# Second sorting of tokens by expert: its products made in four parts between slot tiles

## The chip, the cores and the metric

The kernel runs on one NeuronCore of one Trainium2 chip. A core has five engines that work side by side, each through its own instructions in order: TensorE (PE, matrix products into the accumulator memory PSUM), VectorE (DVE), ScalarE (ACT), GpSimd (POOL, which here issues the indirect transfers), and SyncE (SP, which issues other transfers). They wait for each other through semaphores. The metric is the device time of one execution in microseconds; smaller is better.

## The reference

Two transformer layers run over 2 x 2048 tokens of width 512, each an attention against 128 context rows and a feed-forward part. The change concerns the last part alone, a layer in which each token goes through one of eight experts:

```python
def _L1_ffn_ref(x, Wg, bg, We, be):
    B, S, D, E = (4, 2048, 512, 8)
    probs = jax.nn.softmax(x @ Wg + bg, axis=-1)
    idx = jnp.argmax(probs, axis=-1)
    p = jnp.take_along_axis(probs, idx[..., None], axis=-1)[..., 0]
    e_idx = idx % We.shape[0]
    h = jax.nn.relu(jnp.einsum('bsd,edf->besf', x, We) + be[None, :, None, :])
    onehot = jax.nn.one_hot(e_idx, We.shape[0], dtype=x.dtype)
    out = jnp.einsum('besf,bse->bsf', h, onehot) * p[..., None]
    return out
...
x = x + _L1_ffn_ref(_layernorm(x, axis=-1), ...)
```

The expert of a token is the place of its largest logit, modulo 8; only that expert's result is used.

## The kernel before

The 4096 tokens are 32 token tiles of 128. Instead of all experts for all tokens, the kernel sorts the tokens by expert into slot tiles of 128 slots each, so that a slot tile has one expert, and computes one product of 128x512 by 512x512 for each. Some slots stay empty; 39 slot tiles always suffice. The sorting is done twice: the first covers token tiles 0 to 21 and gives slot tiles 0 to 14, while the attention of the last token tiles still runs; the second covers all 32 token tiles and gives slot tiles 15 to 38. It can begin only when the last token's expert is known, so it runs beside the products of slot tiles 5 to 11.

The function `routing` is a generator that stops at each `yield`; what lies between two of these is called a step here. The steps of the second sorting are:

1. on PE, the rank of each token among those of its expert (`prank`) and the counts (`pcnt`); on VectorE their copies (L1061, L1063)
2. first slot of each expert (L1077 to L1081, "base")
3. the expert of each slot tile, `te` (L1085 to L1092)
4. the slot of each token, split into slot tile and place in it (L1096 to L1102)
5. and 6. the column masks `ohj`, half the token tiles at a time (L1111 to L1118)
7. to 10. the place masks `ohs` for 8 token tiles each: one comparison of 128x1024 elements on VectorE (L1124), the "comparison 1" to "comparison 4" of this text
11. on PE, 32 products (L1132), one per token tile, that add up in one PSUM tile `pid` (128x48) the token number of each slot; on VectorE, from it, the rows for the gather and the output (L1134 to L1138)

Step 11 takes a PSUM tile from a pool of four banks that slot tiles use too.

The order is written by hand, as each engine works through its instructions in program order. The loop over slot tiles at L1322 takes some steps of the sorting and then issues one slot tile, `expert(j)`. Which steps come ahead of which slot tile is in a small table there. `expert(j)` issues, in this order:

- on POOL, the gather of the rows of slot tile j+4 from `x_dram` into one of six buffers (L1149). From j=11 on this needs the rows of the second sorting
- the turning of slot tile j+1: for even tiles by PE (`pt`, L116) and a copy on ScalarE (L1175); for odd tiles above 4 by a transposing transfer that SP has issued earlier (L829) and a copy on ScalarE (L832)
- on PE, the product `pz` of slot tile j (L1185, four blocks, eight matmul records)
- on VectorE, the centring of slot tile j+3 (L104); for odd tiles also the planes for the transposing transfer (L1161, L826)
- on ScalarE, the activation (L1188), on VectorE the sum with the input (L1189), on POOL the indirect output (L1190)

So on VectorE the centring of tile j+3 stands ahead of the sum of tile j, and on ScalarE the copy for tile j+1 ahead of the activation of tile j.

Of the kernel before, what the change touches and what calls it, by code (L numbers as in the profile page):

```python
# [11 lines left out]
F32 = mybir.dt.float32  # L12
# [12 lines left out]
P = 128  # L25
B, S, T, D = 2, 2048, 128, 512
ND = D // P
NT = B * S // P
# [35 lines left out]
def two_layers(ctx: ExitStack, tc: tile.TileContext, a, out):  # L64
    nc = tc.nc
# [85 lines left out]
    with ExitStack() as l0:  # L151
        w0 = l0.enter_context(tc.tile_pool(name="w0", bufs=1))
        psm = l0.enter_context(tc.tile_pool(name="psm", bufs=2, space=PSUM))
# [333 lines left out]
        with tc.manual_schedule(engines={E.PE, E.DVE, E.Activation, E.Pool}):  # L487
# [20 lines left out]
            for u in range(nu + 2):  # L508
# [34 lines left out]
                if g in (0, NG - 1) and u > 1:  # L543
                    if makes and not loaded:
                        load_, args, _, _ = makes[0]
                        loaded.append(load_(*args))
                    elif makes:
                        _, _, make, args = makes.pop(0)
                        turns[u + 1] = make(loaded.pop(), *args)
                        if makes:  # L550
                            load_, args, _, _ = makes[0]
# [85 lines left out]
    with ExitStack() as up:  # L637
        psm = up.enter_context(tc.tile_pool(name="psm_ff", bufs=2, space=PSUM))
# [99 lines left out]
        for blk in range(NT // NBF):  # L738
            for i in range(NI):
                pg = psg.tile([P, BF], F32, name="pg")  # L740
                pu = psg.tile([P, BF], F32, name="pu")
                for w, dst in ((wgT, pg), (wuT, pu)):
                    for c in range(ND):
                        nc.tensor.matmul(  # L744
                            dst, w[:, c, i * P : (i + 1) * P], xqTs[blk][:, c, :],
                            start=(c == 0), stop=(c == ND - 1),
# [13 lines left out]
                n = (blk + 1) * NBF + t  # L760
# [3 lines left out]
                if i >= 3 and i % 2 == 1:  # L764
                    n = (blk + 1) * NBF + (i - 3) // 2
# [18 lines left out]
    psm = l1.enter_context(tc.tile_pool(name="psm_l1", bufs=4, space=PSUM))  # L784
# [31 lines left out]
    scs, xTs, qTs, keeps, ss_, sums, pTs_, os_ = {}, {}, {}, {}, {}, {}, {}, {}  # L816
# [200 lines left out]
    def part(n, shape, dtype=F32, at=0):  # L1017

        size = math.prod(shape)
        v = xw[n][:, at : at + (size * mybir.dt.size(dtype) + 3) // 4]  # L1020
        if dtype is not F32:
            v = v.bitcast(dtype)[:, :size]
        if len(shape) == 1:
            return v
        names = "abc"[: len(shape)]
        return v.rearrange(f"p ({' '.join(names)}) -> p {' '.join(names)}", **dict(zip(names, shape)))
# [6 lines left out]
    def along(k):  # L1033

        return part(16, [NE], at=NE * k)
# [14 lines left out]
    def routing(first):  # L1050

        nt, nj = (NTA, NJA) if first else (NT, NJB)
# [12 lines left out]
        if first:  # L1065
# [3 lines left out]
            start = along(6)  # L1069
# [36 lines left out]
        ohjs, h = [], nt // 2  # L1106
        for q in range(2):
            n0 = q * h
# [8 lines left out]
            )  # L1117
            nc.vector.tensor_scalar(ohj[:, :, 1, :], ones_j, iota_p, None, ALU.mult)  # L1118
            yield
        ohss = []  # L1120
        for n0, n in zip(range(0, nt, 8), (15, 17, 20, 23)):
            h = min(8, nt - n0)
            ohs = part(n, [h, P], BF16)
# [3 lines left out]
            )  # L1127
            ohss += [ohs[:, i] for i in range(h)]
            yield
        pi = psm.tile([P, 2, nj], F32, name="pid", tag="m")  # L1130
        for n in range(nt):
            nc.tensor.matmul(pi, ohss[n], ohjs[n], start=(n == 0), stop=(n == nt - 1))  # L1132
        tokf, pif = part(16, [nj], at=320), part(16, [nj], at=352)
        nc.vector.tensor_scalar(pif, pi[:, 1, :], float(NT * P), None, ALU.add)  # L1134
        nc.vector.scalar_tensor_tensor(tokf, pi[:, 0, :], float(P), pif, ALU.mult, ALU.add)
# [41 lines left out]
    def expert(j):  # L1177

        te, tok, _ = tile_of[j]
        gathered(j + 4)  # L1180
        turned_x2(j + 1)
        e = nc.tensor.value_load(te, min_val=0, max_val=NE - 1)
        pz = psm.tile([P, D], F32, name="pz", tag="m")
        for c in range(ND):
            nc.tensor.matmul(pz, ring[j][:, c, :], we[:, bass.ds(e, 1), c, :], start=(c == 0), stop=(c == ND - 1))  # L1185
        centered_x(j + 3)
        x, acc = xw[j % 6], part(12 + j % 3, [D])
        nc.scalar.activation(acc, pz, AF.Relu, scale=x[:, D + 2 : D + 3])  # L1188
        nc.vector.tensor_tensor(acc, acc, x[:, :D], ALU.add)  # L1189
        nc.gpsimd.indirect_dma_start(  # L1190
            out=out_rows, out_offset=bass.IndirectOffsetOnAxis(ap=tok, axis=0),
            in_=acc, in_offset=None, bounds_check=NT * P - 1, oob_is_err=False,
        )
# [32 lines left out]
    for n in range(NT):  # L1226
# [67 lines left out]
        if n == NTA + 2:  # L1294
            route = routing(True)
# [22 lines left out]
    gated(NT - 1)()  # L1318
    expert(4)
    route = routing(False)  # L1320
    for j in range(5, NJ):
        for _ in range({5: 1, 6: 2, 7: 1, 11: 1}.get(j, 2)):  # L1322
            next(route, None)
        expert(j)
    sched.close()
# [40 lines left out]
```

## Time and profile before

| what | us |
|---|---|
| median of 3 runs | 1606.68 (1604.94 to 1608.51) |
| profiled execution, its own time | 1610.21 |
| its span | 1608.5 |
| PE busy | 1549.8 (96%) |
| VectorE busy | 1194.1 (74%) |
| ScalarE busy | 723.5 (45%) |
| GpSimd busy | 594.3 (37%) |
| second sorting, from the ranks' product to the token rows | 1464.6 to 1493.5 |
| slot tiles 5 to 38 on PE | 1465.7 to 1598.5 |

The profile is of one execution. Its span runs from the first to the last instruction; its own time is 1.7 us longer. In a timeline, each line gives the start and the duration in us, the engine, the source line, the operation, the tiles written and read, and how many instructions were put together; the bracket at the end gives the time for which the engine stood idle before it, and what released it. Matmul records overlap, so a group's end is a little later than the next one's start. A wait for several semaphores is put down to the one that came last by the profile, which can be the wrong one.

The stretch round the second sorting on ScalarE, as a first example of such lines:

```profile
1484.01 0.69 ACT L1188 ACTIVATE x<-pz,x 128x512 f32<-128x512 f32 x1 [2.60 <-PE pz L1185]
1487.31 1.34 ACT L832 COPY x<-x 128x1024 uint16<-128x1024 uint16 x1 [2.61 <-DVE x L104]
1488.52 0.67 ACT L1188 ACTIVATE x<-pz,x 128x512 f32<-128x512 f32 x1
```

These are the activation of slot tile 9, the copy for slot tile 11, and the activation of slot tile 10.

### The profile page before, as it was taken

How to read it: one execution, taken by the hardware profiler on the slowest of the kernel's cores; microseconds unless marked ns; L12 is line 12 of the kernel's file. 1: busy time of each engine (PE TensorE's matmuls, PEld its weight loads, DVE VectorE, ACT ScalarE, POOL GpSimd, SP SyncE). 2: the span in 40 equal slices, each digit the busy share in tenths (PEclk: the TensorE clock that was granted, in tenths of full speed). 3: DMA queues.
4: the chain of work that ended last, by engine and by line, in shares of the span. 5: the costliest groups of instructions: out<-in, count | busy, mean ns of one | idle time of the engine just before them, and what ended most of it. 6: DMA issues, size and time to landing. Idle time of an engine off the chain costs nothing. (4 is left out here: it accounts for less than half of the span.)

```text
span 1608.5 us, 26141 instructions
## 1 busy us (share of the span) xinstructions
PE 1549.8 (96%) x9542; PEld 907.2 (56%) x9542; DVE 1194.1 (74%) x2336; ACT 723.5 (45%) x1537; POOL 594.3 (37%) x576
## 2 busy tenths in 40 slices
PE   7999999999999999999999989999999998999997
PEld 5655555555555556544444456666666665654443
DVE  3467777777777885689986587888888889767442
ACT  1222222222222222244336566777777776753343
POOL 2232222222222221110006653566666443544553
PEclk9999999999999999999999999999999999999999
DMA  9511211211111320466768743122111221114563
GB/s 331 174 37 40 47 40 47 43 53 41 47 40 41 74 43 1 150 171 186 184 167 290 252 159 106 34 47 41 47 47 34 41 41 28 40 47 131 158 162 88
DMA packets 180571, 150.90 MB, mean 94 GB/s; under 512 B 97089, under 2 KB 144665, under 8 KB 180444
## 3 DMA queue, kind: packets, MB, share of 16 engines
q1 hardware_dynamic: 170188, 127.25, 28.3%
q0 software_dynamic: 6240, 18.70, 3.9%
q10 hardware_dynamic: 4016, 3.29, 1.0%
q8 instruction: 76, 1.25, 0.3%
q14 instruction: 51, 0.42, 0.1%
HBM read 89.97 MB, written 41.79 MB: 82 GB/s over the span
## 5 line engine op out<-in xcount | busy, mean ns | idle before, releaser
L419 ACT ACTIVATE pr<-sc 128x1024 f32<-128x1024 f32 x64 | 65.6, 1025 | 421.2 <-PE sc L414 421.1
L393 PE MATMUL pq<-xnT,wq 128*128 128x256 f32 x1024 | 254.4, 391 | 0.0
L451 PE MATMUL pw<-wo,att 128*128 128x512 f32 x512 | 230.8, 593 | 0.0
L393 PEld LDWEIGHTS pq<-xnT,wq 128*128 128x128 f32 x1024 | 184.4, 189 | 67.1 <-issue 44.0
L923 POOL TENSOR_TENSOR s<-s,rs 128x1024 f32<-128x1024 f32 x64 | 132.2, 2075 | 165.4 <-DVE rs L922 165.4
L914 ACT ACTIVATE s<-s,mx 128x128 f32<-128x128 f32 x512 | 175.9, 390 | 29.6 <-DVE mx L905 24.8
L403 POOL TENSOR_TENSOR q<-rt,rt 128x256 f32<-128x256 f32 x64 | 46.7, 729 | 339.7 <-DVE rt L402 335.3
L451 PEld LDWEIGHTS pw<-wo,att 128*128 128x128 f32 x512 | 96.9, 190 | 96.4 <-issue 89.9
L441 DVE RECIPROCAL rd<-sc 128x256 f32<-128x256 f32 x64 | 112.4, 1757 | 46.7 <-PE sc L435 46.7
L1185 PE MATMUL pz<-we,x 128*128 x312 | 140.3, 602 | 2.0 <-ACT x L832 1.7
L872 PE MATMUL pq<-xT,wq 128*128 128x256 f32 x512 | 122.6, 382 | 0.0
L955 PE MATMUL pw<-wo,oT 128*128 128x512 f32 x256 | 115.2, 592 | 1.7 <-issue 1.7
L978 PE MATMUL pl<-wgate,xnT 128*128 128x512 f32 x256 | 116.7, 599 | 0.0
L872 PEld LDWEIGHTS pq<-xT,wq 128*128 128x128 f32 x512 | 96.0, 190 | 33.1 <-issue 20.6
L398 DVE TENSOR_TENSOR rt<-pq,rope_cos 128x256 f32<-128x256 f32 x64 | 27.0, 421 | 104.3 <-PE pq L393 104.3
L749 ACT ACTIVATE gate<-pg,gsc 128x512 f32<-128x512 f32 x88 | 60.7, 689 | 93.5 <-PE pg L744 82.8
L900 DVE SCALAR_TENSOR_TENSOR s<-sc,keep 128x1024 f32<-128x1024 f32 x64 | 78.0, 1219 | 26.9 <-PE sc L892 20.6
L1185 PEld LDWEIGHTS pz<-we,x 128*128 128x128 f32 x312 | 58.2, 192 | 69.6 <-issue 65.9
L92 DVE BATCH_NORM_STATS2 st<-x 128x6 f32<-128x512 f32 x130 | 89.3, 687 | 5.6 <-DMA x<-in_ctx 3.4
L744 PE MATMUL pu<-xqT,wuT 128*128 128x512 bf16 x352 | 90.3, 379 | 2.3 <-DVE h L752 2.2
L744 PE MATMUL pg<-xqT,wgT 128*128 128x512 bf16 x352 | 90.3, 379 | 0.0
L810 PE MATMUL py<-wdT,hb 128*128 128x512 bf16 x352 | 78.8, 383 | 2.2 <-DVE hb L804 1.4
(221 smaller groups left out, 2777.5 us busy)
## 6 DMA issues: line engine op xcount, KB each, us to landing
h_dram<-h SPq DMA_DIRECT2D x88, 256.0 KB
hq<-h_dram SPq DMA_DIRECT2D x31, 704.0 KB
x_dram<-x SPq DMA_DIRECT2D x32, 258.0 KB
x<-in_x SPq DMA_DIRECT2D x32, 256.0 KB
we<-in_L_ffn_We SPq DMA_DIRECT2D x8, 1024.0 KB
xnT<-in_x_turned SPq DMA_DIRECT2D x14, 512.0 KB
along<-stat_dram SPq DMA_DIRECT2D x14, 256.0 KB
w_in<-in_L_ffn_w_gate SPq DMA_DIRECT2D x11, 256.0 KB
```

The source lines that it names most:

```text
L92: nc.vector.bn_stats(out=st, in_=x)
L393: nc.tensor.matmul(pq, wqs[c // 2][:, c % 2, par, g * P : (g + 1) * P], xnTs[k][:, c, :], start=(c == 0), stop=(c == ND - 1))
L441: nc.vector.reciprocal(rd, sc[:, 0, B0:])
L451: nc.tensor.matmul(pw, atts[u][:, f, t * P : (t + 1) * P], wo[:, 2 * g + f, :], start=(g == 0 and f == 0), stop=(g == NG - 1 and f == 1),)
L744: nc.tensor.matmul(dst, w[:, c, i * P : (i + 1) * P], xqTs[blk][:, c, :], start=(c == 0), stop=(c == ND - 1),)
L810: nc.tensor.matmul(py, hbs[n][:, i, :], wdT[:, i, :], start=(i == 0), stop=(i == NI - 1))
L872: nc.tensor.matmul(pq, wq1[:, c, f * P : (f + 1) * P], xTs[blk][:, c, :], start=(c == 0), stop=(c == ND - 1))
L914: nc.scalar.activation(s[:, h, :], s[:, h, :], AF.Exp, bias=mx[:, h : h + 1], **accum)
L923: nc.gpsimd.tensor_tensor(s, s, rs.unsqueeze(2).to_broadcast([P, 8, T]), ALU.mult)
L955: nc.tensor.matmul(pw, os_[n][:, c, :], wo1[:, c, :], start=(c == 0), stop=(c == ND - 1))
L978: nc.tensor.matmul(pl, xn2T[n][:, c, :], wgate[:, c, :], start=(c == 0), stop=(c == ND - 1))
L1185: nc.tensor.matmul(pz, ring[j][:, c, :], we[:, bass.ds(e, 1), c, :], start=(c == 0), stop=(c == ND - 1))
```

## The change

Two things change, both for the second sorting alone.

The 32 products are no longer made together in step 11. After each pause that follows a comparison, the products of the comparisons made before that one are issued: comparison 1's eight products come ahead of comparison 3, comparison 2's ahead of comparison 4, and the rest in step 11. They go into a part of the last token tile's scores in PSUM (its second bank), which nothing uses by then, and not into a tile of the pool. The first sorting does as before.

The table of steps changes as well: ahead of slot tiles 5 to 11 came 1, 2, 1, 2, 2, 2 and 1 steps; now it is 2, 2, 2, 1, 1, 1 and 2. Both need eleven steps and end ahead of slot tile 11, whose gather needs the rows.

```diff
-        ohss = []
+
+        ohss, made = [], 0
+        pi = None if first else scs[NT - 1][:, 1, 0, : 2 * nj].rearrange("p (i j) -> p i j", i=2)
         for n0, n in zip(range(0, nt, 8), (15, 17, 20, 23)):
             h = min(8, nt - n0)
             ohs = part(n, [h, P], BF16)
...
             ohss += [ohs[:, i] for i in range(h)]
             yield
-        pi = psm.tile([P, 2, nj], F32, name="pid", tag="m")
-        for n in range(nt):
-            nc.tensor.matmul(pi, ohss[n], ohjs[n], start=(n == 0), stop=(n == nt - 1))
+            for i in range(made, made if first else n0):
+                nc.tensor.matmul(pi, ohss[i], ohjs[i], start=(i == 0), stop=False)
+                made = i + 1
+        if first:
+            pi = psm.tile([P, 2, nj], F32, name="pid", tag="m")
+        for i in range(made, nt):
+            nc.tensor.matmul(pi, ohss[i], ohjs[i], start=(i == 0), stop=(i == nt - 1))
...
     for j in range(5, NJ):
-        for _ in range({5: 1, 6: 2, 7: 1, 11: 1}.get(j, 2)):
+        for _ in range({8: 1, 9: 1, 10: 1}.get(j, 2)):
             next(route, None)
         expert(j)
```

By source order, VectorE gets comparison 1 ahead of slot tile 8, comparison 2 ahead of 9, comparison 3 ahead of 10 and comparison 4 ahead of 11. PE gets eight products ahead of slot tile 10 and 24 ahead of slot tile 11.

## The prediction

> **What bounds the kernel now.** I read the page first, then the engine timelines of the only stretch that the change touches (the second sorting, 1464 to 1494 us), and last the waits after it.
>
> ```profile
> PE 1549.8 (96%) x9542; PEld 907.2 (56%) x9542; DVE 1194.1 (74%) x2336; ACT 723.5 (45%) x1537; POOL 594.3 (37%) x576
> ```
>
> TensorE is busy 96% of the span, so time is lost where PE stands still. The timeline of PE round the second sorting (start, duration, line, tiles, count, and in brackets the idle time and its releaser):
>
> ```profile
> 1480.37 7.03 PE L1185 MATMUL pz<-we,x 128*128 x16
> 1487.24 0.56 PE L1132 MATMUL pid<-x,x 128*128 128x48 bf16 x16
> 1489.09 0.37 PE L1132 MATMUL pid<-x,x 128*128 128x48 bf16 x8 [1.28 <-DVE x L1124]
> 1490.22 0.37 PE L1132 MATMUL pid<-x,x 128*128 128x48 bf16 x8 [0.76 <-DVE x L1124]
> 1490.44 0.63 PE L116 MATMUL pt<-ident,x 128*128 128x128 f32 x4
> 1491.19 8.78 PE L1185 MATMUL pz<-we,x 128*128 x16
> 1499.81 0.60 PE L116 MATMUL pt<-ident,x 128*128 128x128 f32 x4
> 1500.25 7.03 PE L1185 MATMUL pz<-we,x 128*128 x16
> ```
>
> Each run of 16 pz matmuls is two slot tiles, 7.03 us, or 3.43 a tile from start to start. Between tile 10 (ends at 1487.24) and the transposes for tile 12 (1490.44) stand the 32 matmuls of the sorting: 3.20 us, of which 2.04 is waiting for the third and fourth slot comparison (L1124). The 16 pz after it take 8.78 instead of 7.03: 1.75 us more. The table by stretches says why (columns: stretch, length, PE, PEld, DVE, ACT, POOL, granted clock, DMA share, GB/s):
>
> ```profile
> 1492.00:1493.00 1.00, 1.00 (x2) 0.34 (x1) 0.99 (x3) 0.00 (x0) 0.42 (x1) 0.50 0.26 102
> 1495.00:1498.00 3.00, 3.00 (x8) 1.33 (x7) 1.24 (x2) 1.42 (x2) 0.88 (x1) 1.00 0.70 210
> ```
>
> The clock was 0.50 from about 1491 to 1494.5. So the sorting costs PE 2.04 us of waiting, and 1.75 of half clock behind it. Why the comparisons are late is on VectorE:
>
> ```profile
> 1483.88 0.69 DVE L1189 TENSOR_TENSOR x<-x,x 128x512 f32<-128x512 f32 x1
> 1484.48 2.35 DVE L1124 TENSOR_TENSOR x<-t,x 128x1024 bf16<-128x1024 bf16 x2
> 1486.75 0.54 DVE L104 TENSOR_SCALAR x<-x 128x512 f32<-128x512 f32 x1
> 1487.21 0.69 DVE L1189 TENSOR_TENSOR x<-x,x 128x512 f32<-128x512 f32 x1
> 1487.81 2.35 DVE L1124 TENSOR_TENSOR x<-t,x 128x1024 bf16<-128x1024 bf16 x2
> 1490.65 0.67 DVE L104 TENSOR_SCALAR x<-x 128x512 f32<-128x512 f32 x1 [0.48 <-PE pid L1132]
> ```
>
> VectorE works without a gap here. The last two comparisons stand behind tile 9's sum (L1189), not behind tile 10's. The centring of tile 13 (L104, 1490.65) is put down to PE, but it needs tile 13's gathered rows; those were issued here:
>
> ```profile
> 1484.85 1.75 POOL L1190 DMA_INDIRECT out_x<-x,x  x1 [2.33 <-DVE x L1189]
> 1486.90 1.24 POOL L1149 DMA_INDIRECT x<-x_dram,x  x1 [0.30 <-issue]
> 1489.16 1.90 POOL L1190 DMA_INDIRECT out_x<-x,x  x1 [1.02 <-DVE x L1124]
> ```
>
> The gather of tile 13 (1486.90) ends its issue at 1488.14; 1490.65 is 2.5 us later, as for tiles 14 and 15 (1492.42 to 1495.01, 1495.88 to 1498.50). I read the wait as the landing. Last, the waits from 1500 to 1600 us:
>
> ```profile
> DVE x L104 <- DMA x<-x_dram,x: 51.0, 23, 4.0
> POOL out_x L1190 <- DMA out_x<-x,x: 20.1, 11, 2.5
> ```
>
> From about 1505 VectorE waits for nearly every gather, about 2.2 us each, while PE waits 1.8 us in all. The ring sum, output, gather of the tile five on, centring, sum turns in about 7.57 us per two tiles (outputs at 1503.34 and 1529.84, seven tiles on: 3.79 a tile), PE needs 7.3. The tail follows this ring, and the ring was last started by PE: sums 11 and 12 (1497.30, 1500.73) waited for the activations behind pz 11 and pz 12. What delays pz 11 delays the end.
>
> **What the Trainium skill says.** "TensorE: Matmul & The Clock Gate", Part 1: after an idle window of some 3.4 us the clock is halved, and one busy window restores it; the window runs free. The trace agrees: 0.50 for about 3.4 us after a stretch with 2.04 of 3.20 us waited. "SBUF — State Buffer", "SBUF: two separate sides": VectorE in some modes and GpSimd lock a shared port against each other, and descriptors issued from GpSimd suffer. It fits: the outputs during L1124 took 1.75 and 1.90 us against 1.02 elsewhere. "DMA: Bandwidth & Descriptors", "Anatomy of one DMA": some 2.0 us fixed plus bytes over 436 GB/s; for 128x516 floats, 264 KB, an estimate of 2.6 us. The trace's 2.5 us is used.
>
> **The change part by part.** No instruction goes or comes; the 32 products still cost PE about 0.9 us in all. The bank (the second of the last token tile's scores) has been free since VectorE masked those scores, long before, so I charge nothing; at worst one semaphore wait, below 0.1 us. Leaving the pool of four banks out frees one rotation step: PE waits for no bank here, nothing. What counts is the order. Before, VectorE's steps ahead of tiles 5 to 11 are 1, 2, 1, 2, 2, 2, 1; after, 2, 2, 2, 1, 1, 1, 2. So comparisons 1, 2, 3 and 4 come ahead of tiles 8, 9, 10 and 11, and the fourth now stands behind the centring of tile 13 and the sum of tile 10. The last 8 products, ahead of tile 11 on PE, wait for it.
>
> By hand, with start-to-start costs from the timeline: base 1.73 us, tile experts 0.93, positions 3.02, both column masks 2.97, one comparison 1.14, centring 0.45, centring with planes 1.48 (1.37 for tile 11), sum 0.60.
> - Copies of ranks end at 1466.74, base 1468.47, centring 8; sum 5 waits for its activation (1470.12) and ends the step at 1470.73. Experts and positions to 1474.68, centring 9 to 1476.16, sum 6 to 1476.76, masks to 1479.73.
> - Centring 10 ends at 1480.27. PE wanted it at 1479.94: it starts some 0.4 us late. Tile 9's planes leave 1.3 us later than before (1476.3 against 1475.02); with the same 3.27 us to the copy L832, pz 9 starts near 1480.95 instead of 1480.37. This 0.6 us is swallowed by the later stall.
> - Sum 7 to 1480.78, comparison 1 to 1481.92, centring 11 to 1483.29, sum 8 to 1483.89, comparison 2 to 1485.03.
> - GpSimd: output 7 at 1481.15 to 1482.2-1482.9 (1.02 or 1.75 us), gather 12 to 1483.5-1484.4, output 8 to 1485.3-1486.4, gather 13 to 1486.6-1487.7. Landing 2.5 us later: rows 12 at 1486.0-1486.9, rows 13 at 1489.1-1490.2.
> - VectorE: centring 12 and sum 9 to 1487.1-1488.0, comparison 3 to 1488.2-1489.1, then a wait for rows 13; centring 13 with planes to 1490.6-1491.7, sum 10 to 1491.2-1492.3, comparison 4 done (1.22 us) at 1492.4-1493.5.
> - PE: 8 products ahead of tile 10 (0.22 us, no wait), tile 10 to about 1488.1, 16 products to 1488.5, then idle until 1492.5-1493.6. Before, the last 8 started at 1490.22. Later by 2.3 to 3.4 us; I take 3.0, as the outputs do overlap comparisons.
>
> So two waits of 2.04 us together become one of 4 to 5 us. The half clock stays: an idle stretch longer than a window can hardly go unseen. It costs 1.75 again, or up to a second half window (1.7) more; I take 0.7 more. Queued behind the last products on PE are transposes of tile 12 and pz 11; behind comparison 4 on VectorE the token rows (0.6 us), gather 15 and centring 14. Row and gather 15 come at about 1493.9 (before 1494.90), so they are not late. SP's plane transposes move with L826: tile 9 +1.3, tile 11 -0.5, tile 13 -1.5 to -0.4 us; only tile 9's was seen on PE.
>
> The sum: +3.0 +0.7 = +3.7 us on the profiled execution (1610.21 us, span 1608.5), all of it ahead of pz 11 and so carried by the ring to the end. It would make 1613.9 of that one; the same shift on the median of 1606.68 gives 1610.4. The two differ by 3.5 us already, about the spread of the runs (1604.94 to 1608.51), so about 0.2%, 3.2 us, is what counts as a change.
>
> **The rivals.**
> A, the forecast, late fourth comparison: +2.3 to +5.1, 1609.0 to 1611.8. For it: comparison 4's place behind sum 10, which no landing can lift.
> B, rows 13 come early: if they land before comparison 3 ends, only activation 10 holds: pz 10 ends 1488.1, activation to 1488.9, sum 1489.5, comparison 1490.7. PE restarts +0.5, idle 2.2 us in one piece as now in two; if the free window then doesn't see it, the half clock goes: +0.5 -1.75 = -1.2, 1605.5. This is the case not slower; it decides when gather 13 lands before about 1488.4. Against it: output 8 cannot start before 1484.26, and its 1.02, the gather's 1.3 and 2.5 us give 1489.1.
> C, the ring gains what PE loses: output 11 took 5.07 us to release output 12, and rows 16 landed 4.6 us after their issue against 2.5. If outputs 9 and 10, now 1 to 2 us earlier, clear the queue for these, up to 2.1 us of that and PE's 1.8 of later waits come back: +3.7 -3.9 = -0.2, 1606.5; with the half clock gone too, 1604.7 or below. Against it: output 11 itself starts after pz 11.
> That the products are not split at all is excluded by the instruction order.
>
> **How the numbers follow.** A 0.70, B 0.13, C 0.17. Over +3.2 lie three quarters of A, 0.53, and 0.03 of odd delays in the others: slower 0.56. Faster than -3.2 only what B and C reach with the clock gone and an earlier ring: 0.14. The rest, 0.30, is within 0.2%. Eight in ten: 1605.0 to 1613.0, from C's and B's better halves to A with a full second slow window and some spread; A's own range is 1609.0 to 1611.8.
>
> **What would show it.** Right: one PE idle of 3.5 us or more ahead of the last 8 products, released by the comparison; a DVE wait for x_dram ahead of centring 13; clock 0.50 after it; pz 11 near 1493.5 to 1494.5; and no wait at the first 24 products. Wrong: an idle below 2.3 us there, clock 1.00 throughout, or a tail whose sums 13 and on come earlier against pz 11 than now (before, 9.3 us from activation 11 at 1496.58 to sum 13 at 1505.90).

## The result, and the profile after

The changed kernel took 1612.94 us (median of 6 runs, 1610.97 to 1614.74), the kernel before, run again beside it, 1606.21 (1604.94 to 1608.51). The ratio is 1.0043 (95% interval 1.0033 to 1.0053): slower by 6.7 us between the medians, 6.9 by the ratio, where 3.7 had been forecast. The profiled execution took 1612.53 us, its span 1610.8.

The timeline of PE in the changed kernel, round the second sorting (same columns as before):

```profile
1483.20 0.36 PE L1133 MATMUL sc<-x,x 128*128 128x48 bf16 x8
1483.40 3.68 PE L1191 MATMUL pz<-we,x 128*128 x8
1486.92 0.36 PE L1133 MATMUL sc<-x,x 128*128 128x48 bf16 x8
1487.70 0.37 PE L1133 MATMUL sc<-x,x 128*128 128x48 bf16 x8 [0.42 <-DVE x L1126]
1492.62 0.50 PE L1138 MATMUL sc<-x,x 128*128 128x48 bf16 x8 [4.55 <-DVE x L1126]
1492.95 1.09 PE L116 MATMUL pt<-ident,x 128*128 128x128 f32 x4
1493.98 9.00 PE L1191 MATMUL pz<-we,x 128*128 x16
```

The products are in four groups of eight, as the change says: one ahead of slot tile 10, three behind it. The last group waits 4.55 us for comparison 4, where before there were two waits of 1.28 and 0.76. The 16 pz after it take 9.00 us, against 8.78 in the first profile of before and 7.03 at full clock.

The timeline of VectorE in the changed kernel shows why comparison 4 is late:

```profile
1486.42 1.22 DVE L1126 TENSOR_TENSOR x<-t,x 128x1024 bf16<-128x1024 bf16 x1
1489.14 0.55 DVE L104 TENSOR_SCALAR x<-x 128x512 f32<-128x512 f32 x1 [1.50 <-DMA x<-x_dram,x]
1489.72 0.38 DVE L1167 TENSOR_SCALAR x<-x 128x4 f32<-128x4 f32 x1
1490.13 0.69 DVE L826 COPY x<-x 128x1024 uint16<-128x1024 uint16 x1
1490.74 0.68 DVE L1195 TENSOR_TENSOR x<-x,x 128x512 f32<-128x512 f32 x1
1491.35 1.22 DVE L1126 TENSOR_TENSOR x<-t,x 128x1024 bf16<-128x1024 bf16 x1
```

Comparison 3 is done at 1487.64. Then VectorE stands still for 1.50 us until the rows of slot tile 13 land, centres that tile, makes its planes, adds up tile 10, and only then makes comparison 4. Before, VectorE had no gap there and made comparison 4 ahead of all this.

The table by stretches for the changed kernel (stretch, length, PE, PEld, DVE, ACT, POOL, granted clock, DMA share, GB/s):

```profile
1491.00:1492.00 1.00, 0.00 (x0) 0.00 (x0) 1.00 (x2) 0.00 (x0) 0.29 (x1) 0.50 0.67 219
1495.00:1496.00 1.00, 1.00 (x3) 0.48 (x2) 0.00 (x0) 0.00 (x0) 0.57 (x1) 0.50 0.00 0
1498.00:1499.00 1.00, 1.00 (x4) 0.43 (x3) 0.00 (x0) 0.00 (x0) 0.00 (x0) 1.00 0.00 0
```

The number after POOL's is the clock: it is 0.50 already while PE still waits, and is back at 1.00 only near 1497.8. PE worked about 5 us at half speed.

### The profile page after: what moved, and what is told of

It reads as the page before. It is cut to its first block, busy times and chain, and to the rows that moved or that the text cites. A ratio compares the mean times of both kernels' runs of the same rounds, so it can differ in the third digit from the quotient of the medians.

```text
span 1610.8 us, 26141 instructions
## 1 busy us (share of the span) xinstructions
PE 1549.5 (96%) x9542; PEld 906.6 (56%) x9542; DVE 1196.3 (74%) x2336; ACT 721.6 (45%) x1537; POOL 593.3 (37%) x576
## 5 line engine op out<-in xcount | busy, mean ns | idle before, releaser
L914 ACT ACTIVATE s<-s,mx 128x128 f32<-128x128 f32 x512 | 175.2, 388 | 29.2 <-DVE mx L905 24.4
```

The costliest lines, as they stand in the source:

```text
L914: nc.scalar.activation(s[:, h, :], s[:, h, :], AF.Exp, bias=mx[:, h : h + 1], **accum)
```

## How executions are compared here

The second sorting starts with the ranks' product (L1056). Over all profiles it started between 1463.2 and 1468.2 us, although nothing ahead of it differs in any kernel below. That scatter of 5 us has nothing to do with the change, and it is about as large as the effect. So the profiles are compared from this product on: to the transposes for slot tile 12 (PE is past the sorting), to those for tile 14 (past the slow clock), and to the end of the span. All in us, read from the PE timelines and the spans. The last column gives the ratio of the times to those of the kernel before, run on the same chip, with its 95% interval:

| kernel | to tile 12 | to tile 14 | to the end | half clock behind the sorting | timed against before |
|---|---|---|---|---|---|
| before, first profile | 25.8 | 35.2 | 143.9 | yes | |
| before, `x1_before_again` | 25.3 | 33.0 | 141.4 | no | 0.9999 (0.9990 to 1.0009) |
| before, `z1_before_b` | 25.9 | 33.6 | 141.8 | no | |
| before, `z2_before_c` | 25.6 | 33.3 | 144.3 | no | |
| changed | 29.8 | 39.6 | 147.6 | yes | 1.0043 (1.0033 to 1.0053) |
| changed, `y1_after_again` | 29.2 | 39.4 | 148.3 | yes | 1.0035 (1.0023 to 1.0046) |
| `x4_table_only` | 29.2 | 38.8 | 147.7 | yes | 1.0037 (1.0025 to 1.0049) |
| `y2_split_only` | 28.0 | 35.5 | 145.4 | ahead of tile 12 | 1.0011 (1.0004 to 1.0019) |
| `y3_c4_early_split` | 26.4 | 34.2 | 144.6 | no | 1.0001 (0.9993 to 1.0010) |
| `x3_fill_after` | 29.6 | 36.9 | 146.0 | no | 1.0030 (1.0018 to 1.0042) |
| `x2_fill_before` | 25.9 | 33.6 | 143.5 | no | 1.0000 (0.9992 to 1.0007) |
| `y4_all_early` | 24.0 | 31.8 | 142.2 | no | 1.0000 (0.9990 to 1.0011) |
| `z3_deep_gather` | 25.4 | 33.2 | 144.1 | no | 1.0015 (1.0008 to 1.0022) |
| `z4_deep_all_early` | 24.0 | 31.8 | 146.3 | no | 1.0017 (1.0010 to 1.0023) |

## The experiments

### Which part of the change costs it

The theory was the forecast's own: comparison 4 now stands behind the sum of slot tile 10. The rivals were the split products with their bank, and the earlier steps of the sorting. Three kernels part them.

The table alone, on the kernel before:

```diff
-        for _ in range({5: 1, 6: 2, 7: 1, 11: 1}.get(j, 2)):
+        for _ in range({8: 1, 9: 1, 10: 1}.get(j, 2)):
```

> The new table of steps alone: the 32 products together ahead of slot tile 11, in a bank of the pool as before. Theory 'it is comparison 4's place behind the sum of slot tile 10': as slow as the changed kernel, 1612.9 within 1 us, with PE idle about 4.3 us ahead of the last eight products. Rival 'the split products or their bank cost it': near the kernel before, below 1608.

It took 1614.69 us beside 1608.79 for the kernel before on that chip, ratio 1.0037. On its PE timeline the products stand together again, and the wait is there as well, 3.50 us after one of 1.01:

```profile
1491.59 0.56 PE L1132 MATMUL pid<-x,x 128*128 128x48 bf16 x16
1493.17 0.37 PE L1132 MATMUL pid<-x,x 128*128 128x48 bf16 x8 [1.01 <-DVE x L1124]
1497.04 0.50 PE L1132 MATMUL pid<-x,x 128*128 128x48 bf16 x8 [3.50 <-DVE x L1124]
1498.25 8.82 PE L1185 MATMUL pz<-we,x 128*128 x16
```

So the table alone makes the loss, within the intervals all of it; neither the four parts nor the bank are needed for it. The long wait is shorter than the 4.3 us expected, the two together are 4.5. The absolute time was above the 1 us band that was written down, because the kernel before was 2.6 us higher on this chip too; the ratio is what agrees.

The split alone, the changed kernel with the old table (the diff above reversed):

> The products in four parts in the scores' bank, with the old table of steps. Theory 'only the places of the comparisons count': comparison 2 is made late, so PE waits ahead of slot tile 10 (about 2.5 us) and hardly ahead of tile 11; in sum about 0.5 us later than before at tile 11, so within 0.1% of before. Rival 'the split itself costs the 4 to 7 us': as slow as the changed kernel.

Ratio 1.0011 (1.0004 to 1.0019), about 1.8 us slower and at the edge of the 0.1% expected. PE waits at another place:

```profile
1485.11 0.37 PE L1133 MATMUL sc<-x,x 128*128 128x48 bf16 x8 [1.44 <-DVE x L1126]
1486.24 0.50 PE L1133 MATMUL sc<-x,x 128*128 128x48 bf16 x8 [0.76 <-DVE x L1126]
1487.08 4.92 PE L1191 MATMUL pz<-we,x 128*128 x8 [0.34 <-issue]
```

These are the groups of comparisons 1 and 2 ahead of slot tile 10. With the old table those comparisons are not made yet, so PE stands 2.2 us there, and tile 10 runs at half clock in part (4.92 us against 3.6). In exchange the last 16 products wait for nothing. Tile 12 comes 2.3 us later than the mean of before (25.67), not 0.5: the half clock in tile 10, 1.3 us of it, had been left out of the expectation. Splitting the products brings the wait forward; it doesn't shorten it by itself.

The changed kernel with comparison 4 one place earlier:

```diff
-        for _ in range({8: 1, 9: 1, 10: 1}.get(j, 2)):
+        for _ in range({8: 1, 9: 1, 11: 1}.get(j, 2)):
```

> The changed kernel with one edit: comparison 4 is made together with comparison 3 ahead of slot tile 10, so it stands behind the sum of tile 9 and not of tile 10 (table 2, 2, 2, 1, 1, 2, 1). Theory 'comparison 4 behind sum 10 costs it': the idle ahead of tile 11 falls below 1 us, PE waits about 1 us for comparison 2 ahead of tile 10, no half clock: 4 us or more faster than the changed kernel, same as or up to 2 us faster than before. Rival 'the earlier steps (masks ahead of tile 7) delay the tiles': still over 2 us slower than before.

Ratio 1.0001 (0.9993 to 1.0010): the whole loss is gone with one step moved. Its PE timeline:

```profile
1488.44 0.37 PE L1133 MATMUL sc<-x,x 128*128 128x48 bf16 x8 [0.37 <-DVE x L1126]
1489.75 3.70 PE L1191 MATMUL pz<-we,x 128*128 x8 [0.94 <-issue]
1493.28 0.36 PE L1133 MATMUL sc<-x,x 128*128 128x48 bf16 x8
1493.87 0.37 PE L1138 MATMUL sc<-x,x 128*128 128x48 bf16 x8 [0.22 <-DVE x L1126]
```

The last wait is 0.22 us. The masks ahead of tile 7 and the split are still as in the changed kernel, so the rival that these delay the tiles falls as well. It is not faster than before, though: PE now loses 0.37 and 0.94 us ahead of tile 10.

### What the half clock adds

The changed kernel unchanged, on the chip of the runs above:

> The changed kernel, unchanged, on the same chip as the three below. Timed 0.25 to 0.45% slower than before (about 4 to 7 us). The profile again shows one idle of 4 to 5 us ahead of the last eight products and the half clock behind it; from the ranks' product to the transposes for tile 14 about 39.6 us.

Nearly as expected: 1615.78 us beside 1609.88, ratio 1.0035, and half clock behind the wait; the wait is in two pieces, 3.49 us ahead of the last eight products after one of 0.95. From the transposes for tile 12 to those for tile 14 it took 10.15 us, the first profile 9.86; at full clock the same stretch takes 7.69 (`x1_before_again`). Against that, the half clock costs 2.2 to 2.5 us there, and a further 0.1 in the last products and transposes ahead of it.

To take the clock's part away and leave the wait, five 128x512 fp32 products into an unused bank fill it, in the changed kernel:

```diff
+        for _ in range(0 if first else 5):
+            nc.tensor.matmul(scs[NT - 1][:, 2].rearrange("p c k -> p (c k)"), ident, we[:, 0, 0, :], start=True, stop=True)
         for i in range(made, nt):
```

> The changed kernel with five such products (4.3 us) in the 4.55 us in which PE waits for comparison 4. The wait stays; the clock should stay at 1.00. Theory 'one late comparison, and the half clock behind it': 2.4 to 2.7 us faster than the changed kernel, about 1610.4, and still 4 us slower than before. Rival 'the clock is no part of it, the tail takes it up': as the changed kernel, 1612.9.

```profile
1490.16 4.54 PE L1138 MATMUL sc<-we,ident 128*128 128x512 f32 x10
1494.53 0.36 PE L1140 MATMUL sc<-x,x 128*128 128x48 bf16 x8
1494.74 0.64 PE L116 MATMUL pt<-ident,x 128*128 128x128 f32 x4
1495.21 7.03 PE L1193 MATMUL pz<-we,x 128*128 x16
```

The 16 pz take 7.03 us again and the clock is 1.00. The filling ran 0.7 us longer than the wait, which here ended at 1493.8; still tile 14 comes 2.6 us earlier than the mean of the two profiles of the changed kernel (36.9 against 39.5), and the end 1.9 us earlier. The time says less: 1.0030 (1.0018 to 1.0042) against 1.0035 and 1.0043 is 0.8 to 2.1 us faster where 2.4 to 2.7 had been expected, and the intervals overlap. So the clock's part is shown in the profile, and the timed runs neither confirm nor refute its size.

The same in the kernel before, one product ahead of comparison 3's and one ahead of comparison 4's:

```diff
         for n in range(nt):
+            if not first and n in (16, 24):
+                nc.tensor.matmul(scs[NT - 1][:, 2].rearrange("p c k -> p (c k)"), ident, we[:, 0, 0, :], start=True, stop=True)
             nc.tensor.matmul(pi, ohss[n], ohjs[n], start=(n == 0), stop=(n == nt - 1))
```

> The kernel before with one 128x512 fp32 product (0.86 us, into a bank nothing reads) ahead of comparison 3's and one ahead of comparison 4's products, where PE waits 1.28 and 0.76 us. The waits stay, the idle time falls below 0.5 us. If the half clock of 1.75 us is there in the timed executions of the kernel before: 1.3 to 1.75 us faster, about 1604.7, and clock 1.00 behind the sorting. If it is only in the profiled one: same as before within 0.3 us.

Ratio 1.0000 (0.9992 to 1.0007): no gain. That fits a half clock that is mostly absent in the kernel before, which the next runs show directly.

### What the kernel before really does there

> The kernel before, unchanged, for a second profile of it. Timed: ratio 1.000 within 0.1%. Theory 'clock differs between executions' (the half clock behind the second sorting is there in some executions of the kernel before and not in others): this profile may show clock 1.00 from 1491 to 1494.5 and then a profiled time 2 us or so below 1610.21. Rival 'the excess of the first profile lies ahead of the sorting': the stretch from the ranks' product to the transposes for tile 14 again takes about 35.2 us with the half clock in it, and the 3 to 4 us by which the first profile lay above the median are found before 1464 us.

> The kernel before, unchanged, a third profile. So far one of two profiles of it had the half clock behind the products (from the ranks' product to the transposes for tile 14: 35.2 us with it, 33.0 without). If it is chance where the window falls, this one has either; if the first profile was the odd one, 33 us.

> The kernel before, unchanged, a fourth profile, with the same question as the third.

None of the three has the half clock. The third profile (`z1_before_b`) is the telling one, as its waits are as long as those of the first:

```profile
1490.83 0.37 PE L1132 MATMUL pid<-x,x 128*128 128x48 bf16 x8 [1.36 <-DVE x L1124]
1491.96 0.37 PE L1132 MATMUL pid<-x,x 128*128 128x48 bf16 x8 [0.76 <-DVE x L1124]
1492.18 0.64 PE L116 MATMUL pt<-ident,x 128*128 128x128 f32 x4
1492.90 7.13 PE L1185 MATMUL pz<-we,x 128*128 x16
```

2.12 us of waiting, and the 16 pz at full speed; the first profile waited 2.04 us and had 8.78. So with two us of idle time in two pieces the half clock comes in some executions (one of four here) and not in others. With 4.4 to 5.0 us, in two pieces too, it came in each of the three profiles that left the wait unfilled.

What differs is where the waits fall on a time grid. Each trace records when the granted clock changes. Within one trace, any two of these moments are a whole multiple of 3.413 us apart, to within 4 ns; from one execution to the next, this grid lies differently over the work. Cut into windows along the grid (same columns as in the table by stretches above), the first profile of before gives:

```profile
1487.72:1491.13 3.41, 1.31 (x24) 0.88 (x20) 2.93 (x4) 1.47 (x2) 2.32 (x2) 1.00 0.31 90
1491.13:1494.55 3.42, 3.36 (x4) 1.51 (x5) 2.23 (x8) 0.69 (x1) 2.03 (x2) 0.50 0.57 168
```

and `z1_before_b`:

```profile
1487.45:1490.87 3.42, 2.06 (x22) 0.98 (x21) 3.42 (x5) 1.82 (x2) 2.13 (x2) 1.00 0.61 148
1490.87:1494.28 3.41, 2.56 (x23) 1.51 (x24) 2.97 (x5) 0.75 (x2) 2.95 (x2) 1.00 0.35 135
```

In the first, both waits fall into one window, PE is busy for only 1.31 us of it, and the next window has the half clock. In `z1_before_b` a boundary of the grid lies between the two waits; PE is busy for 2.06 and 2.56 us, and the clock stays. The same cut over all 14 profiles, from 30 to 1585 us, finds 43 windows at full clock that have the half clock in the next one. PE was busy for at most 1.77 us in each of them; between 1.52 and 1.77 us the clock dropped in some windows and stayed in others, and every full-clock window with more work was followed by full clock. In the changed kernel the long wait spans a boundary:

```profile
1487.56:1490.97 3.41, 0.37 (x8) 0.27 (x8) 1.84 (x5) 0.78 (x2) 1.99 (x2) 1.00 0.49 156
1490.97:1494.38 3.41, 1.76 (x13) 1.46 (x14) 2.67 (x7) 0.24 (x1) 1.75 (x1) 0.50 0.78 182
```

The second of these windows is itself at half clock, and PE still works for only 1.76 us in it. Another window at half clock follows (in the 14 profiles that happened after half-clock windows with up to 2.65 us of work), so the clock is low for 6.83 us and not for 3.41. The Trainium skill ("TensorE: Matmul & The Clock Gate", Part 1) describes such a free-running window of some 3.4 us, and the traces agree. It names an idle window as what halves the clock; here the clock was halved after windows in which PE worked for up to 1.77 us, and the measurement decides.

### Can another order beat both?

If the wait costs, making the comparisons early enough should pay. With the products together as before, all comparisons two tiles earlier:

```diff
-        for _ in range({5: 1, 6: 2, 7: 1, 11: 1}.get(j, 2)):
+        for _ in range({10: 0, 11: 1}.get(j, 2)):
```

> The products together as before, with all four comparisons two tiles earlier (table 2, 2, 2, 2, 2, 0, 1): comparisons 1 and 2 ahead of tile 8, 3 and 4 ahead of tile 9. Theory: no wait and no half clock at the products, 2 to 3.8 us less than before on PE at tile 11; if the tail keeps that, 0.1 to 0.2% faster than before. Rival 'the tail's ring of gather, centring, sum and output sets the end': the gain at tile 11 is there but gone at the last tile, same as before.

```profile
1490.13 0.97 PE L1132 MATMUL pid<-x,x 128*128 128x48 bf16 x32
1490.94 0.63 PE L116 MATMUL pt<-ident,x 128*128 128x128 f32 x4
1491.73 7.13 PE L1185 MATMUL pz<-we,x 128*128 x16 [0.17 <-ACT x L832]
```

All 32 products run without a wait, in 0.97 us, and tile 12 comes at 24.0 us, 1.7 before the mean of the kernel before. But the ratio is 1.0000 (0.9990 to 1.0011), which leaves room for 1.6 us at most: by the median the gain is lost on the way to the end, as the rival had it.

Two more kernels asked which link of the tail swallows it. From slot tile 15 on, the rows of a tile are gathered six tiles ahead instead of four, into twelve buffers (`xw` 26 to 31 and 0 to 5) instead of six:

```diff
+    def rows(j):
+        return xw[j % 6] if j < NJA else xw[(26 + (j - NJA) % 12) % 32]
...
-        gathered(j + 4)
+        for i in [j + 4] if j < 11 else [2 * j - 7, 2 * j - 6] if j < 13 else [j + 6]:
+            gathered(i)
```

> The kernel before with the gathers six slot tiles ahead instead of four from slot tile 13 on, into buffers that are free by then. Theory 'the ring of gather, centring, sum and output paces the tail': VectorE's waits for gathered rows (51 us from 1500 to 1600) nearly go, the pairs of tiles come to 7.3 to 7.4 us instead of 7.6, 2 to 3.5 us faster than before. Rival 'the outputs' wait for the output before them paces it': same as before.

The waits of this kernel from 1500 to 1600 us:

```profile
POOL out_x L1194 <- DMA out_x<-x,x: 27.3, 16, 3.2
ACT x L1192 <- DMA out_x<-x,x: 16.8, 6, 3.2
DVE x L104 <- DMA x<-x_dram,x: 7.0, 9, 1.0
```

VectorE's waits for rows fell from 51.0 us in the first profile of before to 7.0, and PE started its last pair of tiles 121.7 us after the ranks' product (124.4 to 127.2 in the four profiles of before). Yet the end came no earlier, and the time is 1.0015 (1.0008 to 1.0022), slower. Now the outputs wait for the outputs before them, and the activations for those to free their buffers. The timeline of POOL at the end of this kernel:

```profile
1586.37 1.00 POOL L1194 DMA_INDIRECT out_x<-x,x  x1 [3.24 <-DMA out_x<-x,x]
1589.86 0.99 POOL L1194 DMA_INDIRECT out_x<-x,x  x1 [2.49 <-DMA out_x<-x,x]
1593.27 0.98 POOL L1194 DMA_INDIRECT out_x<-x,x  x1 [2.42 <-issue]
1596.13 0.98 POOL L1194 DMA_INDIRECT out_x<-x,x  x1 [1.88 <-DMA out_x<-x,x]
1598.99 0.98 POOL L1194 DMA_INDIRECT out_x<-x,x  x1 [1.88 <-issue]
```

PE ends its last product at 1594.7, but the outputs still follow each other every 2.9 to 3.5 us, the last at 1601.84. Three of these five waits are put down to the landing of the output before; the other two, of nearly the same lengths, are put down to nothing that the profile shows (`issue`). With the comparisons early as well:

> Deep gathers together with all comparisons two tiles earlier, which put slot tile 11 on PE 1.5 to 2 us earlier than before without a gain at the end. If the ring swallowed that gain, both together are faster than the deep gathers alone by up to 2 us, 0.2 to 0.35% faster than before. Rival 'outputs pace it': same as before.

1.0017 (1.0010 to 1.0023): no better. No kernel here beats the kernel before. That the outputs' waits for each other hold the end is thus argued from the traces: no kernel without these waits was tried.

## Why the prediction was right in its mechanism and wrong in its size

- **The place.** Right: comparison 4 behind the centring of tile 13 and the sum of tile 10, one long idle ahead of the last eight products, VectorE waiting for the rows of tile 13. `x4_table_only` makes it, `y3_c4_early_split` takes it away.
- **The restart, "I take 3.0" (2.3 to 3.4).** Measured from the ranks' product to the last eight products: 29.42 and 28.90 us in the changed kernel, 25.60, 25.12, 25.68 and 25.43 before, so 3.7 later by the means. Too small by 0.7. The range's top, 3.4, was passed too. In the first profile of the changed kernel, the centring of tile 11 itself waited 0.32 us for its rows and ran 0.83, so sum 8 started 0.6 us later than in the hand timeline, and output 8 and gather 13 behind it. The forecast also had no wait in the first 24 products, while the third group waited 0.42 us.
- **The half clock, "It costs 1.75 again ... I take 0.7 more."** This is the step that failed. It set the changed kernel against one execution that happened to have the half clock, and so took the 1.75 as part of the base. Three of four profiles of before have none. From the transposes for tile 12 to those for tile 14 the four took 9.37, 7.69, 7.68 and 7.69 us (mean 8.1), the two of the changed kernel 9.86 and 10.15 (mean 10.0). With the 0.1 just ahead of it, 2.0 us are added by the means, not 0.7. Together with the 3.7 of the restart this is the 5.7 us by which tile 14 comes later. That an idle stretch longer than the window would be seen was right, and so was the second half window, which came in all three profiles with the late comparison 4 left unfilled; what was not asked is whether 2.04 us in two pieces is always seen.
- **From the profile to the median.** "The same shift on the median of 1606.68" was the same error in another form. On the two first profiles from the ranks' product to the end the forecast was exact (147.6 against 143.9, 3.7), but by luck: at tile 14 they were 4.4 apart, and the tail took 0.7 back. Against the mean of four profiles of before (142.8, from 141.4 to 144.3) and two of the changed kernel (148.0) the shift is 5.1 us, which is near the timed 5.6 (1.0035) and 6.9 (1.0043).
- **The tail carries it.** At tile 14 the shift is 5.7 us by the means, at the end 5.1. The tail did carry a delay nearly whole, as forecast. In the other direction it does not: `y4_all_early` was 2.0 us earlier at tile 14 and the same at the end, by time. The forecast had named gather, centring, sum and output as the ring. In `z3_deep_gather` the gathers' waits are nearly gone and the end is no earlier, so the ring alone doesn't set it; what stays there are the outputs' waits for each other, which no run took away.
- **Rivals.** B (rows 13 early) did not happen: they landed 2.38 us after the end of their issue, as the 2.5 had it. C (the tail gives it back) hardly happened: between tile 14 and the end about half a us came back by the means, less than the ends scatter, and the sum of tile 13 came 9.09 us after the activation of tile 11, before 9.32.

## What to carry to other kernels

A step of a helper engine that PE waits for has to be placed by what stands ahead of it in its own queue: moved behind an instruction that itself needs PE's last result and a transfer, it makes PE wait for both. Before the effect of an idle stretch on the clock is taken from a profile, see in further executions whether it is always there; a cost that only some executions pay is not part of the base. And a delay at the head of a self-timed tail is passed on, while a gain of the same size may be lost to the next link, so test the two directions apart. That last point rests here on one late and one early order.

## What the runs showed of the hardware that was not expected

- In each of the 14 traces the granted clock changed only on a grid of 3.413 us. From 1.00 it fell to 0.50 after windows of this grid in which PE was busy for at most 1.77 us, and never after one with more work. So 2.12 us of waiting, split by a boundary of the grid, left the clock at 1.00 (`z1_before_b`), while 2.04 us within one window brought 3.41 us of half clock (first profile of before).
- With 4.4 to 5.0 us of waiting (the three profiles with the late comparison 4 left unfilled) the clock fell each time, and stayed low for two such windows, 6.83 us.
- Filling a wait with products that nothing reads kept the clock at 1.00 (`x3_fill_after`), and brought tile 14 2.6 us forward by the profile.
- Indirect outputs of 128 rows of 512 floats, which waited mostly for the one before to land, followed each other in 2.9 to 3.5 us at the end of `z3_deep_gather`, with no gather between them.
